# LSTM state as the loaded operand: four 32-column tiles of TensorE, with the gates' weights moving

## The chip, the cores and the metric

The kernel runs on one core of a Trainium2 chip. The core has TensorE (PE in the profile; its loads of the stationary operand are shown apart, as PEld), VectorE (DVE), ScalarE (ACT), GpSimd (POOL) and SyncE (SP), which here issues most transfers. The metric is the device time of one execution in microseconds. Before the change the median of three runs is 1354.62 us (1354.28 to 1355.16); the profiled execution took 1354.57 us, and its span from first to last instruction is 1352.8 us.

## What is computed

`x` has the shape (32, 512, 128): 32 batches of 512 nodes with 128 features. `adj` is (32, 512, 512), symmetric, of zeros and ones. Four graph layers follow each other, each after a LayerNorm and a ReLU and each added to `x`:

- layer 0: attention masked by `adj`;
- layer 1: a graph convolution whose last weight matrix comes from an LSTM;
- layer 2: four small layers with sums over neighbours in both directions;
- layer 3: a product with one weight matrix, a sum over neighbours, a bias and a PReLU.

The change is in layer 1. A convolution of the last 128 nodes of each batch gives a sequence of T = 128 steps with 128 features for each of the 32 batches, and the LSTM runs over it:

```python
def step(carry, xt):
    h, c = carry
    z = xt @ w_ih.T + b_ih + h @ w_hh.T + b_hh
    i, f, g, o = jnp.split(z, 4, axis=-1)
    c = jax.nn.sigmoid(f) * c + jax.nn.sigmoid(i) * jnp.tanh(g)
    h = jax.nn.sigmoid(o) * jnp.tanh(c)
    return ((h, c), h)
...
out = jax.nn.sigmoid(jnp.matmul(agg, lw))
```

`lw` is the LSTM's output, 128x128 for each batch, so layer 1 of every batch needs the last step. A step is a product of the 32x128 state with a 128x512 weight matrix, a few element-wise operations on 32x128 numbers, and the next step waits for them.

## The kernel before

**Stages.** Pass 1 (`pass_1`) runs for all 32 batches up to the convolution: attention for the last 128 nodes only, then the sequence goes to the tile `seq` (f_seq, 128 features on partitions x 128 steps x 32 batches). Then the LSTM (`lstm`) runs. Pass 2 (`pass_2`) does the attention of the other 384 nodes, batch by batch, and does not need the LSTM: scores (line 1256), exponentials (1259), the multiply with `adj` (1260) and the values (1265), with the query product in line 1247. `rest` does layers 1 to 3 of a batch. It can start with squares of `adj` (1317), a normalised copy of its input and a first sum over neighbours (the tile f_pg, line 1301); from line 1353, where the LSTM's result of that batch is transposed, it needs the last step. `fold` prepares weights of layer 2 between pass 2's batches.

**Order.** Nothing here is left to the order of the source. Each piece is handed to a planner (`Plan`) with an engine, a duration, a rank and what it reads and writes. `Plan.run` simulates the engines with these durations and starts, on each engine, the piece that can start first; among those that can start together the lower rank wins. The instructions are then issued in that order on each engine, and on the chip each engine works through its own queue in order. The LSTM's pieces have ranks 0 to 127, which is below `URGENT`; pass 2 has 20,000 and more, `rest` 30,000 and more. While an urgent piece is foreseen on an engine (`foresee`, `expected`), a piece of higher rank is not started if it would run into it by more than 0.2 us (line 689). Pieces of `rest` and the last `LATE` = 3 batches of pass 2 have ranks that mix them in the final stage, but nothing keeps them from starting earlier if their buffers are free. Some buffer tags are handed out strictly in the order of creation ("ar", "x", "n0" and others); the tag "mm" stands for the eight banks of PSUM.

**The LSTM's layout.** The partitions hold the features of a gate and the free axis holds the 32 batches. For each gate q the weights `w[:, W_HH + q, :]`, 128x128, are loaded and the state `seq[:, t - 1, :]`, 128x32, moves (`states`, line 1193). In fp32 each such product leaves two records of loading and two of multiplying in the profile. Gates i, f and g of four steps share one PSUM tile f_z; gate o of sixteen steps has a tile of its own, f_zo. Before use both are filled with the biases (`fill`, lines 913 and 917), and the products of the inputs are added for all steps of the tile at once (`inputs`, line 1186). A step is then:

- PE: three products of the state into f_z, then the one of gate o into f_zo (1193);
- ACT: tanh of i, f, g (1208) and of o (1225); sigmoids are computed as tanh of half the argument, and the weights and biases have been scaled for that by `halves`;
- DVE: `cell`, three instructions (1215 to 1217), gives the new cell state f_c;
- ACT: tanh of f_c (1228);
- DVE: the product with gate o is written into `seq[:, t, :]` (1229), in place of the input that is no longer needed, and the next step's products read it from there.

The biases `lstm_b` are loaded as 8 rows, turned to columns by a PE transpose (line 933), summed and scaled, and spread to `lb_row`.

Of the kernel before, what the change touches and what calls it, by code (L numbers as in the profile page):

```python
# [520 lines left out]
class Plan:  # L521
# [19 lines left out]
    def __init__(self, bufs, fifo, banks):  # L541
        self.banks = banks
        self.last = float("inf")
        self.sealed = 0
        self.ops = []
        self.bufs = bufs
        self.made = {}
        self.fifo = {t: [] for t in fifo}
# [40 lines left out]
    def run(self, tc, queues):  # L589
# [14 lines left out]
        for o in ops:  # L604
            if o.rank >= self.last:
                k, sub = divmod(o.rank - self.last, 10)
                o.rank = self.last + 12 * k - 9 * max(0, k - 28) + 200.0 - (min(behind[o], 60) if sub == 5 else behind[o] + (70 if sub == 2 else 0.0))
        free = {}
# [24 lines left out]
        def foresee(o):  # L633

            at, before = o.end, o.engine
            for _ in range(5):
                o = min((n for n in o.next if n.rank < self.URGENT), key=lambda n: n.no, default=None)
                if o is None:
                    return
                (e, (took, _)), = o.engines.items()  # L640
                at += self.lag(before, e, True)
                before = e
                expected[e] = at
                at += took
# [7 lines left out]
        def room(o):  # L652

            at = 0.0
            need = {}
            for c in o.cells:
                if c not in seen:
                    if c.tag in self.fifo and self.fifo[c.tag][turn[c.tag] + need.get(c.tag, 0)] is not c:
                        return None
                    need[c.tag] = need.get(c.tag, 0) + 1  # L660
            for t, n in need.items():
                if len(slots[t]) < n:
                    return None
                at = max(at, sorted(slots[t])[n - 1])
            return at
# [5 lines left out]
        while done < len(ops):  # L671
            best = None
            for e, cands in pools.items():
                first = None
                held = expected.get(e)
                for rank, no, o in cands:
# [10 lines left out]
                    if rank < self.URGENT:  # L687
                        held = s
                    elif held is not None and s < held < s + o.engines[e][0] - 0.2:
                        continue  # L690
# [14 lines left out]
            for c in o.cells:  # L705
# [7 lines left out]
                if c.left == 0:  # L713
                    slots[c.tag].append(c.free_at)
                    if c.tag == self.banks:
                        unused.append((c.free_at, c.place))
            for n in o.next:
                n.waits -= 1
                if n.waits == 0:
                    put(n)  # L720
# [9 lines left out]
def symmetric(ctx, tc, x, adj, weights, cols, rows, lstm_b, prelu_a, out, fail):  # L730
# [19 lines left out]
    LATE = 3  # L750
    FOLDS = (4, 7, 10, 13)
    MOVED = range(2, B - 2)
    TURN = 32
    assert D == P and N == 512

    BUFS = {"a": 2, "ar": 6, "x": 7, "xn": 5, "y": 5, "gs": 5, "inv": 4, "n0": 4, "n1": 4, "n2": 4, "n3": 4, "low": 3, "hp": 2, "dt": 2, "mm": 8, "st": 4, "mv": 4, "rs": 4, "sh": 4, "dg": 4, "dv": 4,
            "ri": 3, "th": 3, "c": 3, "cu": 2, "cv": 2, "tcn": 2}
# [99 lines left out]
    lbc = const.tile([P, 4], FP, name="f_lbc")  # L857
# [8 lines left out]
    lb = const.tile([8, P], FP, name="f_lb")  # L866
# [20 lines left out]
    w_lb = load(HEAD + 100, 4, lb, lstm_b.rearrange("s q f -> (s q) f"))  # L887
# [37 lines left out]
    def halves(q):  # L925
        half = 1.0 if q == 2 else 0.5
        nc.gpsimd.tensor_scalar_mul(w[:, W_HH + q, :], w[:, W_HH + q, :], 0.5 * half)
        if q != 2:
            nc.gpsimd.tensor_scalar_mul(w[:, W_IH + q, :], w[:, W_IH + q, :], half)
            nc.gpsimd.tensor_scalar_mul(lbc[:, q : q + 1], lbc[:, q : q + 1], half)  # L930
    lbs = plan.fixed(lbc)
    pb8 = bank("f_pb8", (P, 2, 4), whole=False)
    PE(HEAD + 110, T_TR, lambda: nc.tensor.transpose(pb8.t, lb, ident[0:8, 0:8]), [w_lb], [pb8])

    def two_biases():
        nc.vector.tensor_copy(lbc, pb8.t[:, 0, :])
        nc.vector.tensor_add(lbc, lbc, pb8.t[:, 1, :])
    DVE(HEAD + 110, 0.3, two_biases, [pb8], [lbs])
    for q in range(4):
        POOL(HEAD + 110, 0.6 if q == 2 else 1.4, lambda q=q: halves(q), [w_lstm], [lbs])  # L940
    lb_row = const.tile([P, 4 * B], FP, name="f_lb_row")
    lbrs = plan.fixed(lb_row)
    DVE(HEAD + 110, t_dve(P), lambda: nc.vector.tensor_copy(lb_row.rearrange("p (q b) -> p q b", b=B),
                                                      lbc.unsqueeze(2).to_broadcast([P, 4, B])), [lbs], [lbrs])
# [227 lines left out]

    def lstm():
        last = list(conv_ops)
        steps = []
        c = None

        def inputs(t, n, gates, name, ahead):

            g = len(gates)  # L1180
            z = bank(f"f_z{name}_{t}", (P, n, g, B), filled=True)
            row = lb_row[:, gates[0] * B : (gates[-1] + 1) * B]
            fill(2_000 + t, lambda: z.t.rearrange("p k q b -> p k (q b)"), row.unsqueeze(1).to_broadcast([P, n, g * B]), [lbrs],
                 z, conv_ops + steps[t - ahead : t - ahead + 1] if t >= ahead else conv_ops)
            for i, q in enumerate(gates):
                PE(2_000 + t, t_mm(n * B), lambda i=i, q=q: nc.tensor.matmul(
                    z.t[:, :, i, :], w[:, W_IH + q, :], seq[:, t : t + n, :], start=False, stop=(i == g - 1),
                    skip_group_check=True), [], [z])
            return z

        def states(z, k, gates, t):
            for i, q in enumerate(gates):
                nc.tensor.matmul(z.t[:, k, i, :], w[:, W_HH + q, :], seq[:, t - 1, :], start=False, stop=True,  # L1193
                                 skip_group_check=True)

        z = zo = None
        for t in range(T):
            R = t
            k = t % MANY
            if k == 0:  # L1200
                z = inputs(t, MANY, (0, 1, 2), "", MANY + 1)
            if t % (4 * MANY) == 0:
                zo = inputs(t, 4 * MANY, (3,), "o", 3)
            ko = t % (4 * MANY)
            if t:
                PE(R, 0.65, lambda z=z, k=k, t=t: states(z, k, (0, 1, 2), t), [], [z], after=last)
            th = new("th", (P, 4, B), f"f_th_{t}")
            ACT(R, 0.22, lambda th=th, z=z, k=k: nc.scalar.activation(th.t[:, :3, :], z.t[:, k, :, :], AF.Tanh), [z], [(th, 0)])  # L1208
            cn = new("c", (P, B), f"f_c_{t}")
            if t:  # L1210
                u = new("cu", (P, B), f"f_cu_{t}")
                v = new("cv", (P, B), f"f_cv_{t}")
# [10 lines left out]
            if t:  # L1223
                PE(R, 0.22, lambda zo=zo, ko=ko, t=t: states(zo, ko, (3,), t), [], [zo], after=last)
            ACT(R, 0.13, lambda th=th, zo=zo, ko=ko: nc.scalar.activation(th.t[:, 3, :], zo.t[:, ko, 0, :], AF.Tanh), [zo],
                [(th, 1)])
            tcn = new("tcn", (P, B), f"f_tcn_{t}")
            ACT(R, 0.13, lambda tcn=tcn, c=c: nc.scalar.activation(tcn.t, c.t, AF.Tanh, scale=0.5), [c], [tcn])
            last = [DVE(R, 0.09, lambda th=th, tcn=tcn, t=t: nc.vector.scalar_tensor_tensor(  # L1229
                seq[:, t, :], th.t[:, 3, :], 1.0, tcn.t, OP.add, OP.mult), [th, tcn], [])]  # L1230
# [277 lines left out]
    plan.last = 30_000  # L1508
# [84 lines left out]
```

## Time and profile before

| | before |
|---|---|
| median of three runs | 1354.62 us |
| PE busy over the span | 1329.0 us (98%) |
| DVE, ACT, POOL busy | 74%, 58%, 28% |
| mean granted clock of TensorE | 0.996 |
| LSTM, start of first tanh to start of last state | 187.0 to 509.3 us |
| line 1193, records of loading and multiplying | 1016 each |

A row of the costliest groups names the line, the engine, the operation, the tile written and the tiles read, the shapes and the count; then busy time and the mean duration; then the idle time of the engine just before, with what ended it:

```profile
L1193 PE MATMUL f_z<-f_seq,f_w 128*128 128x32 f32 x762 | 98.4, 266 | 0.4 <-DVE f_seq L1229 0.2
L1208 ACT ACTIVATE f_th<-f_z 128x96 f32<-128x96 f32 x128 | 32.0, 250 | 78.2 <-PE f_z L1193 75.3
```

The first row is the state's products for gates i, f and g: 127 steps, three gates and two records are 762. "128*128" is the part of the array that is used and 128x32 the result. PE did not stand idle ahead of them. The second row is the first tanh of each of the 128 steps, 250 ns long; of the time that ACT stood idle ahead of it, 75.3 us ended when PE had finished the products. The durations of matmuls overlap: PE takes up the next one before the last has come out at the other end, so a sum of durations is more than the time that PE was occupied.

### The profile page before, as it was taken

To read this page: it belongs to the slowest core of one execution; us is meant where nothing else is said; L and a number is where in the kernel's file an instruction comes from. 1 tells how busy PE (TensorE), PEld (TensorE's weight loads), DVE (VectorE), ACT (ScalarE), POOL (GpSimd) and SP (SyncE) were. 2 spreads that over 40 slices of the span, in tenths; PEclk is the share of its full clock that TensorE was granted. 3 is DMA by queue.
4 is the path that set the end of the run, shared out by engine and by line. 5 is a ranking of instruction groups with operands and counts; after the bars stand their busy time and mean duration, and the time that the engine had idled before them with its cause. 6 is when DMAs were issued, how large, how long until landed. Compare 5 with 4: busy or idle time off the path is not lost. (4 is left out here: it accounts for less than half of the span.)

```text
span 1352.8 us, 24316 instructions
## 1 busy us (share of the span) xinstructions
PE 1329.0 (98%) x8016; PEld 1078.1 (80%) x8018; DVE 1004.6 (74%) x3315; ACT 782.5 (58%) x1905; POOL 374.2 (28%) x689
## 2 busy tenths in 40 slices
PE   8999999999999999999999999999999999999996
PEld 6888888888888887787787787787787787787774
DVE  7988866566666678768778778788788788788644
ACT  5666644454444556566666566566566666676433
POOL 4645421111111224333233233233232232242101
PEclk9999999999999999999999999999999999999999
DMA  8888888656555535856656755756655656674211
GB/s 242 280 273 275 285 278 299 216 169 190 170 176 173 161 89 131 185 112 130 150 121 134 150 123 133 156 117 134 155 122 135 150 125 134 147 145 98 47 32 35
DMA packets 286120, 215.74 MB, mean 159 GB/s; under 512 B 135576, under 2 KB 248480, under 8 KB 285984
## 3 DMA queue, kind: packets, MB, share of 16 engines
q1 hardware_dynamic: 269088, 197.32, 53.1%
q0 software_dynamic: 16896, 16.78, 7.9%
q8 instruction: 65, 1.06, 0.3%
q14 instruction: 71, 0.58, 0.2%
HBM read 125.84 MB, written 56.75 MB: 135 GB/s over the span
## 5 line engine op out<-in xcount | busy, mean ns | idle before, releaser
L1301 PE MATMUL f_pa<-f_ar,f_y 128*128 128x512 f32 x1024 | 304.5, 431 | 0.0
L1301 PEld LDWEIGHTS f_pa<-f_ar,f_y 128*128 128x128 f32 x1024 | 190.2, 189 | 73.6 <-issue 40.1
L1407 PE MATMUL f_py<-f_wf,f_n 128*128 128x128 f32 x1280 | 174.1, 275 | 0.0
L1407 PEld LDWEIGHTS f_py<-f_wf,f_n 128*128 128x128 f32 x1280 | 164.8, 192 | 8.7 <-ACT f_n L1422 1.0
L1422 ACT ACTIVATE f_n<-f_pa,f_bcol 128x512 f32<-128x512 f32 x128 | 88.3, 690 | 132.1 <-PE f_pa L1418 131.9
L1418 PE MATMUL f_pa<-f_n,f_wf 128*128 128x512 f32 x320 | 152.8, 592 | 0.0
L1375 POOL DMA_DIRECT2D f_das<-f_ar x32 | 36.0, 1126 | 367.6 <-DVE f_ar L1344 348.6
L1283 ACT CAST f_y<-f_py 128x512 fp32r<-128x512 f32 x128 | 74.4, 581 | 78.7 <-PE f_py L1407 55.2
L1265 PE MATMUL f_po<-f_v,f_e 128*128 128x129 f32 x768 | 108.7, 279 | 1.5 <-DMA f_v<-f_dv 1.5
L1265 PEld LDWEIGHTS f_po<-f_v,f_e 128*128 128x128 f32 x768 | 98.8, 191 | 14.1 <-issue 2.7
L1193 PEld LDWEIGHTS f_z<-f_seq,f_w 128*128 128x128 f32 x762 | 96.7, 191 | 15.6 <-DVE f_seq L1229 12.7
L1414 DVE TENSOR_TENSOR f_pa<-f_pa,f_inv 128x512 f32<-128x512 f32 x128 | 88.3, 692 | 17.4 <-PE f_pa L1301 17.2
L1284 DVE TENSOR_TENSOR f_y<-f_py,f_y 128x512 fp32r<-128x512 f32 x128 | 87.0, 681 | 18.3 <-ACT f_y L1283 18.0
L1256 PE MATMUL f_s<-f_q,f_kq 128*128 128x384 f32 x256 | 99.9, 500 | 0.0
L1193 PE MATMUL f_z<-f_seq,f_w 128*128 128x32 f32 x762 | 98.4, 266 | 0.4 <-DVE f_seq L1229 0.2
L1418 PEld LDWEIGHTS f_pa<-f_n,f_wf 128*128 128x128 f32 x320 | 58.0, 189 | 46.2 <-issue 37.4
L1025 ACT ACTIVATE f_xn_c<-f_x,f_sh_c,f_rs_c 128x128 f32<-128x128 f32 x199 | 86.1, 495 | 11.9 <-DVE f_sh_c L1033 11.9
L1380 DVE SCALAR_TENSOR_TENSOR f_junk<-f_a,f_aT 128x1024 bf16<-128x1024 f32 x64 | 78.3, 1223 | 9.7 <-DMA f_aT<-f_das 8.1
L1317 ACT ACTIVATE f_ar<-f_a 128x512 fp32r<-128x512 f32 x128 | 78.8, 620 | 8.4 <-DMA f_a<-in_adj_dram 6.3
L1276 POOL COPY f_ln<-f_mv_r 128x3 f32<-128x3 f32 x32 | 9.5, 296 | 264.0 <-DVE f_mv_r L1007 255.0
L1260 DVE TENSOR_TENSOR f_e<-f_e,f_a 128x384 f32<-128x384 f32 x128 | 68.5, 551 | 14.4 <-ACT f_e L1259 13.4
L1208 ACT ACTIVATE f_th<-f_z 128x96 f32<-128x96 f32 x128 | 32.0, 250 | 78.2 <-PE f_z L1193 75.3
(204 smaller groups left out, 2921.4 us busy)
## 6 DMA issues: line engine op xcount, KB each, us to landing
f_a<-in_adj_dram SPq DMA_DIRECT2D x32, 1024.0 KB
f_a<-in_adj_dram SPq DMA_DIRECT2D x32, 768.0 KB
f_das<-f_ar POOLq DMA_DIRECT2D x32, 512.0 KB, 5.1
f_dkq<-f_kh SPq DMA_DIRECT2D x32, 448.0 KB
f_kq<-f_dkq SPq DMA_DIRECT2D x32, 448.0 KB
f_dv<-f_v SPq DMA_DIRECT2D x32, 258.0 KB
f_v<-f_dv SPq DMA_DIRECT2D x32, 258.0 KB
f_x<-in_x_dram SPq DMA_DIRECT2D x32, 256.0 KB
```

The lines of the kernel that those rows point to most:

```text
L1025: nc.scalar.activation(xn.t[:, t, :], xc.t[:, t, :], AF.Relu, bias=shift(t), scale=rstd(t))
L1193: nc.tensor.matmul(z.t[:, k, i, :], w[:, W_HH + q, :], seq[:, t - 1, :], start=False, stop=True, skip_group_check=True)
L1256: PE(R, t_mm(NR), lambda s=s, j=j: nc.tensor.matmul(s.t, kq.t[:, bass.ts(j, P)], q.t, start=True, stop=True), [kq, q], [s])
L1265: PE(R, t_mm(P), lambda t=t, j=j: nc.tensor.matmul(po.t[:, t, :], es[j].t[:, bass.ts(t, P)], v.t[:, j, :], start=(j == 0), stop=(j == NT - ...
L1284: DVE(rank, t_dve(N), lambda: nc.vector.tensor_sub(parts.t[:, :, 1, :], src.t, f32(parts.t[:, :, 0, :])), [src, (parts, 0)], [(parts, 1)])
L1301: nc.tensor.matmul(pg.t, parts.t[:, j, k, :], ar.t[:, j, :], start=(k == 0 and j == 0), stop=(k == 1 and j == NT - 1))
L1317: ACT(R, 0.62, lambda t=t: nc.scalar.activation(ar.t[:, t, :], a.t[:, t, :], AF.Square, accum_out=deg.t[:, t : t + 1]), [a], [(ar, t), (de ...
L1380: nc.vector.scalar_tensor_tensor(junk, flat(a.t[:, 2 * k : 2 * k + 2, :]), 1.0, flat(aT.t[:, 2 * k : 2 * k + 2, :]), OP.mult, OP.not_equal ...
L1407: nc.tensor.matmul(py.t[:, j, :], nodes[n].t[:, bass.ts(j, P)], wf[:, W_F[i] + c, 0, :], start=False, stop=(c == nch - 1), skip_group_chec ...
L1414: before = DVE(R, t_dve(N), lambda pa=pa: nc.vector.tensor_mul(pa.t, pa.t, inv_row.t), [inv_row], [pa])
L1418: nc.tensor.matmul(pa.t, wf[:, W_F[i] + c, 1, :], nodes[n].t, start=False, stop=(c == nch - 1), skip_group_check=True)
L1422: ACT(R, 0.57, lambda pa=pa, n=n, i=i: nc.scalar.activation(n.t, pa.t, AF.Tanh, bias=bcol[:, i : i + 1]), [pa], [n])
```

## The change

The two operands of the LSTM's products change places. The state, 128 features x 32 batches, is now loaded, and the gates' weights move. A loaded operand of 32 columns fills a quarter of the array's columns, so the array is used as four tiles of 32 columns. Tile j gets the same state and the weights of features 32j to 32j+31 of all four gates, 128 moving columns, and writes PSUM partitions 32j to 32j+31. So partitions hold (block of features, batch), and the free axis holds 4 gates x 32 features of the block; the element-wise operations keep their size, 128x32. All four gates of four steps share one tile f_z, and f_zo is gone.

The new state comes out in that layout (f_h), while the next step has to load it with features on partitions. A DVE transpose by blocks of 32x32 turns it and writes `seq[:, t, :]`.

The inputs' products can't be done for four steps at once with this layout, since each step's input would be another loaded operand. They are done by the same function, one step's worth behind the state's products of each step, for the tile that comes next. The biases now lie along the free axis and are loaded in that form; the PE transpose of the biases is gone, and sums and scaling go to POOL.

The purpose is to use the array's columns fully for a state with only 32 batches, and so to need less of PE for each step. The planner gets new durations (0.26 us for a set of four tiles, 0.1 for switching), `LATE` becomes 2, the threshold for pieces that run into an urgent one becomes 0.05 us, and one PSUM bank is kept free of pass 2 and later pieces until the LSTM has ended (`spared`, `left`).

```diff
-                    elif held is not None and s < held < s + o.engines[e][0] - 0.2:
+                    elif held is not None and s < held < s + o.engines[e][0] - 0.05:
...
-                if len(slots[t]) < n:
+                if len(slots[t]) < n + (t == self.banks and o.rank >= self.spared and self.left > 0):
...
-    LATE = 3
+    LATE = 2
...
+    T_STEP, T_SWITCH = 0.26, 0.1
...
-        def states(z, k, gates, t):
-            for i, q in enumerate(gates):
-                nc.tensor.matmul(z.t[:, k, i, :], w[:, W_HH + q, :], seq[:, t - 1, :], start=False, stop=True,
-                                 skip_group_check=True)
...
+        def products(z, k, m, h):
+            for j in range(P // TURN):
+                part = bass.ts(j, TURN)
+                nc.tensor.matmul(z.t[part, k, :, :], h, w[:, m : m + 4, part], start=False, stop=True, skip_group_check=True)
...
+            def step(z=z, coming=coming, k=k, t=t):
+                if t:
+                    products(z, k, W_HH, seq[:, t - 1, :])
+                if coming is not None:
+                    products(coming, k, W_IH, seq[:, t + MANY, :])
...
-            last = [DVE(R, 0.09, lambda th=th, tcn=tcn, t=t: nc.vector.scalar_tensor_tensor(
-                seq[:, t, :], th.t[:, 3, :], 1.0, tcn.t, OP.add, OP.mult), [th, tcn], [])]
+            h = new("h", (P, TURN), f"f_h_{t}")
+
+            def out_of(th=th, tcn=tcn, h=h, t=t):
+                nc.vector.scalar_tensor_tensor(h.t, th.t[:, 3, :], 1.0, tcn.t, OP.add, OP.mult)
+                nc.vector.transpose(seq[:, t, :], h.t)
+            last = [DVE(R, 0.31, out_of, [th, tcn], [h])]
```

## The prediction, made before the changed kernel was run

> **What bounds the kernel now.** The chain that ended last is cut off after two DVE instructions, so it says nothing. I read the busy time by stretches first, for 186 to 510 us, where the LSTM runs beside pass 2 (first f_z tanh at 187.0, last state written at 509.3).
>
> ```profile
> 292.00:346.00 54.00, 53.84 (x387) 46.23 (x385) 34.79 (x161) 25.69 (x92) 5.97 (x12) 1.00 0.62 186
> 346.00:400.00 54.00, 54.00 (x382) 46.43 (x382) 35.20 (x161) 25.64 (x90) 7.79 (x15) 1.00 0.57 174
> ...
> 510.00:560.00 50.00, 47.77 (x263) 37.17 (x262) 41.29 (x117) 32.59 (x79) 18.14 (x26) 0.97 0.62 137
> 560.00:760.00 200.00, 198.45 (x1074) 156.50 (x1073) 153.33 (x399) 126.38 (x282) 62.08 (x93) 1.00 0.61 137
> ```
>
> Columns: stretch and length; PE, PEld, DVE, ACT, POOL busy with counts; clock; DMA share; GB/s. PE is full with the LSTM and after it; DVE stands at 0.65, ACT at 0.48 and DMA at 0.6. Next, the timeline of one step (the work between it left out):
>
> ```profile
> 383.71 0.19 DVE L1229 SCALAR_TENSOR_TENSOR f_seq<-f_th,f_tcn 128x32 f32<-128x32 f32 x1 [0.35 <-ACT f_tcn L1228]
> ...
> 384.09 0.75 PEld L1193 LDWEIGHTS f_z<-f_seq,f_w 128*128 128x128 f32 x6
> 384.20 0.75 PE L1193 MATMUL f_z<-f_seq,f_w 128*128 128x32 f32 x6
> 384.76 0.30 PEld L1193 LDWEIGHTS f_zo<-f_seq,f_w 128*128 128x128 f32 x2
> ...
> 384.99 0.25 ACT L1208 ACTIVATE f_th<-f_z 128x96 f32<-128x96 f32 x1 [0.68 <-PE f_z L1193]
> ...
> 385.27 0.19 DVE L1215 SCALAR_TENSOR_TENSOR f_cu<-f_th,f_c 128x32 f32<-128x32 f32 x1 [0.76 <-ACT f_th L1208]
> 385.38 0.18 DVE L1216 SCALAR_TENSOR_TENSOR f_cv<-f_th 128x32 f32<-128x32 f32 x1
> ...
> 385.60 0.19 DVE L1217 SCALAR_TENSOR_TENSOR f_c<-f_cu,f_cv 128x32 f32<-128x32 f32 x1
> 385.88 0.23 ACT L1228 ACTIVATE f_tcn<-f_c 128x32 f32<-128x32 f32 x1 [0.47 <-DVE f_c L1217]
> ...
> 386.14 0.19 DVE L1229 SCALAR_TENSOR_TENSOR f_seq<-f_th,f_tcn 128x32 f32<-128x32 f32 x1 [0.35 <-ACT f_tcn L1228]
> ```
>
> From state to state 2.43 us pass: 0.38 to the first weight load, 0.90 to the tanh, 0.28 + 0.33 + 0.28 + 0.26 through the cell. The mean step is (509.3 − 188.0)/127 = 2.53. So **two limits lie 4% apart**: the chain of a step, and PE.
>
> PE's work in the window, by spacing of starts rather than by busy time (which overlaps): a pair of load and matmul with up to 128 moving columns takes (0.75 − 0.19)/5 = 0.112 us; one with 384 columns 0.323 (sixteen at 514.6 last 5.33, the last 0.49); with 512, 0.43. The window holds 1016 pairs of line 1193 (113.8 us), 192 and 16 of line 1186 (21.5 + 6.9), 662 of line 1265 (74.1), 275 of lines 1256 and 1247 (88.8), and folds and two early aggregates (about 14). The sum is 319 of 324 us, 142 of it the LSTM's. One batch of pass 2 is 24 × 0.112 + 10 × 0.323 = 5.9 us; 60 pairs of line 1265, 2.5 batches, fall after 510.
>
> **What the Trainium skill says.** "TensorEngine Tiling (Array Packing)", Tiling Modes, Key Properties: the tiles load and multiply in parallel, but a change of tiling mode drains TensorE. The trace of before has no tiles, so it shows neither. "TensorE: Matmul & The Clock Gate", LDWEIGHTS (loading the stationary operand): a load takes its columns divided by 1.2, in ns, so 107 for 128; the 112 ns spacing agrees. It would be 27 for 32 columns, which no row here shows. Same page, Measured speedup vs the span model: three column tiles of 32 gave 2.38×. "VectorE: DVE Perf Modes", The three transpose paths: DVE turns 32x32 blocks only, which is all the new layout needs.
>
> **The change part by part.** *Set of four tiles.* A product of the state had 4 gates × 2 records = 8 pairs, 0.90 us. It becomes 4 tiles × 2 records, again 8 pairs, each with 32 loaded and 128 moving columns. Bounds: a pair of 128 moving columns takes 0.112, so all four side by side leave 2 × 0.112 = 0.22, and none 0.90 (16 instructions at 56 ns is also what line 1193 shows, and I can't tell whether loading or issue sets that). At the page's 2.38/3 = 0.79 per tile, four give 3.2 and 0.90/3.2 = 0.28 us. I take 0.28.
>
> *Input products.* 192 + 16 pairs, 28.4 us, become 128 more sets, queued behind the state products in the same piece, so behind the instruction that the tanh waits for: PE time, not chain.
>
> *Mode switches.* Two a step. Bounds: 0, and 0.38 (twice 0.19, the shortest duration of a 32-column matmul, as its way through the array). I take 0.15, half of it ahead of the products. The LSTM on PE is then 255 × 0.28 + 127 × 0.15 = 71 + 19 = 90 us instead of 142: **52 us of PE work less**.
>
> *Chain, products.* Load to tanh is now 5 × 0.112 + 0.34. New: 7 × 0.035 + 0.34 + 0.08 (276 − 191 ns, median 128-column against shortest 32-column matmul) − 0.07 (shorter first load) + 0.07 switch = 0.67, a saving of 0.23.
>
> *Chain, turning back.* The state goes to f_h and a DVE transpose writes f_seq, and the products now wait for that one. Dependent DVE instructions start 0.22 apart (line 1216 to 1217), and the nearest row for the transpose is
>
> ```profile
> L1387 DVE STREAM_TRANSPOSE f_dT<-f_dinv 128x32 f32<-128x32 f32 x32 | 6.5, 204 | 0.0
> ```
>
> so +0.22 on the chain and 26 us more DVE in the window (0.65 to about 0.74, hidden). Behind it on DVE stand only pass 2's multiplies, which have slack. The o gate's products came last and now come with the others; its tanh runs behind the first tanh as before: nothing. Bias fills: 25 + 7 of 384 and 8 of 512 columns become 32 of 512, on engines at half load: nothing. Bias loads and sums at the head lie beside pass 1, whose PE is 96% busy: nothing. So the undisturbed step stays at 2.43 − 0.23 + 0.22 = **2.42 us**.
>
> *Disturbance.* Now 2.53 − 2.43 = 0.10 a step, from pieces of pass 2 that hold an engine when the chain's turn comes (PE's load stood idle only 31 times for the state, so mostly it came to a busy PE). The threshold for starting such a piece falls from 0.2 to 0.05 us and PE gets slack; DVE gets more work. I take 0.05: 127 steps of 2.47 are 313 us instead of 127 × 2.53 = 321, **8 us less**.
>
> *What fills PE.* A window of 316 us (three more for its ends, as now) holds 90 (LSTM) + 14 + up to 212 us of pass 2, 35 batches; only 30 are left when it begins. So the 2.5 batches after 510 can move in: LATE goes from 3 to 2, and later ranks too are started where an engine would idle. That is worth up to 2.5 × 5.9 = 14.7 us, of which I take 10. Two more early aggregates (16 pairs at some 0.2, half a fp32 pair of 512 columns): about 4 us; more must wait for the LSTM's end, since line 1353 turns its result. The rest of the kernel stays full and unchanged. Sum: 8 + 10 + 4 = 22, so 1354.6 − 22 = 1332.6, **1332 us**.
>
> **Rivals.** *A: all freed PE time is used.* PE 98% busy speaks for it; against it, 2.42 × 127 = 307 us of chain, above PE's 90 + 14 + 30 × 5.9 = 281. It needs a shorter step (2.3, if switches cost nothing and disturbance vanishes) plus more early work: 1354.6 − 52 = 1303.
>
> *B: the tiles overlap badly.* If the second record of a tile waits for its first and the tiles follow in program order, a set takes 5 × 0.107 = 0.54; the step becomes 2.47 + 0.26 = 2.73, its 127 take 347 us, +26, less the 10 and 4 that still move: 1367, slower. Without any overlap (0.90), the LSTM is 255 × 0.90 + 19 = 249 us of PE, +107, about 1455. For it: 56 ns per instruction is the closest spacing that this trace shows for fp32. Against: the page's 2.38×.
>
> *C: nothing net.* The chain grows by 0.1 (dear switches): 127 × 2.57 = 326, +5, against 14 that moves: 1346. To end level with before it must grow by 14/127 = 0.11 over 2.53, so by 0.17 over my 2.47.
>
> **How the numbers follow.** My forecast (spread 1314 to 1348, C included) has 0.66; A 0.13; B 0.17; an even result 0.04. Predicted: 1332. Below 1304 lies half of A, and above 1364 some two thirds of B, so 1304 to 1364 leaves out under 2 in 10. Faster: 0.66 + 0.13 = 0.79; same 0.04; slower 0.17.
>
> **What would show it.** The eight pairs of a set start within 0.28 us (B: 0.54 or 0.90). Load to tanh 0.67. The transpose starts 0.22 after the write of f_h, takes about 204 ns, and releases PE. Step 2.47 in the mean, LSTM over near 502 us. PE in the window at about 0.95 instead of full, DVE 0.74; fewer than 30 pairs of the value product after the LSTM's end. I am wrong if the set is above 0.4 us, if a switch costs more than 0.2, or if the late batches stay behind the LSTM.

## The result, and the profile after

The changed kernel takes 1338.9 us (median of 4 runs, 1337.5 to 1342.4) against 1354.9 (1354.3 to 1356.5, 4 runs) for the kernel before on the same chip. The ratio is 0.9884, with a 95% interval from 0.9863 to 0.9905: **16 us faster**, 7 us less of a gain than the 22 to 23 of the prediction. The profiled execution is the longest of the four (1342.4; its span is 1340.5), so its stretches are a few us longer than those of the median.

The head of the page, after. The digits are tenths of busy time and of the granted clock in 40 slices of 33.5 us:

```profile
PE 1287.5 (96%) x8829; PEld 994.2 (74%) x8830; DVE 1013.2 (76%) x3416; ACT 780.5 (58%) x1921; POOL 368.2 (27%) x689
...
PE   8999999999999937999999999999999999999996
...
PEclk9999999999999967999999999999999999999998
```

PE's busy time fell by 1329.0 − 1287.5 = 41.5 us, but the span by only 12.3: 29.2 us more of it are idle. The digits 3 and 7 say where, and the clock fell in the same two slices. The stretches (columns as in the prediction: stretch and length; PE, PEld, DVE, ACT, POOL; clock; DMA share; GB/s):

```profile
346.00:400.00 54.00, 53.84 (x575) 36.34 (x568) 42.47 (x203) 27.73 (x103) 8.89 (x18) 1.00 0.72 218
440.00:476.00 36.00, 35.89 (x380) 24.77 (x379) 27.95 (x136) 20.96 (x76) 11.33 (x20) 1.00 0.34 90
476.00:510.00 34.00, 11.79 (x116) 7.22 (x115) 16.04 (x63) 12.50 (x49) 3.51 (x8) 0.60 0.59 116
510.00:560.00 50.00, 45.06 (x251) 36.72 (x250) 39.15 (x115) 32.67 (x75) 17.62 (x29) 0.93 0.51 110
560.00:760.00 200.00, 200.00 (x1069) 156.81 (x1068) 151.86 (x393) 123.93 (x273) 53.68 (x83) 1.00 0.58 128
```

Beside the LSTM PE is as full as before, until pass 2 runs out at 476. From there to the LSTM's end (last transpose at 504.4) it has the steps and nothing else. In the stretch from 476 to 510 it is busy for 11.79 of 34 us, at a clock of 0.60, where it was full before. That stretch alone holds 22.2 of the 29.2 us. From 560 us on PE is as full as before.

The row groups of the new products and of the transpose:

```profile
L1193 PE MATMUL f_z<-f_w,f_seq 128*32 128x128 f32 x2040 | 84.1, 283 | 22.2 <-DVE f_seq L1241 16.5 <-ACT f_ar L1329 4.5
L1241 DVE STREAM_TRANSPOSE f_seq<-f_h 128x32 f32<-128x32 f32 x128 | 27.0, 211 | 4.8
```

PE now does stand idle for the state (16.5 us, more than half of it in one wait that is shown below; before it was 0.2). One step in the middle of pass 2, from the timeline, other work left out:

```profile
381.58 0.16 DVE L1240 SCALAR_TENSOR_TENSOR f_h<-f_th,f_tcn 128x32 f32<-128x32 f32 x1
381.77 0.21 DVE L1241 STREAM_TRANSPOSE f_seq<-f_h 128x32 f32<-128x32 f32 x1
...
382.04 0.38 PEld L1193 LDWEIGHTS f_z<-f_w,f_seq 128*32 128x32 f32 x16 [0.64 <-DVE f_seq L1241]
382.04 0.64 PE L1193 MATMUL f_z<-f_w,f_seq 128*32 128x128 f32 x16
...
382.53 0.25 ACT L1219 ACTIVATE f_th<-f_z 128x96 f32<-128x96 f32 x1
...
382.61 0.30 PEld L1268 LDWEIGHTS f_s<-f_q,f_kq 128*128 128x128 f32 x2 [0.20 <-issue]
...
383.72 0.19 DVE L1240 SCALAR_TENSOR_TENSOR f_h<-f_th,f_tcn 128x32 f32<-128x32 f32 x1
```

Read it as follows. Sixteen pairs (a set for the state, a set for a later step's input) take 0.64 us, the last one 0.27, so they start (0.64 − 0.27)/15 = 0.025 us apart in the mean. That mean hides a pattern. The same view cut off at 382.10 shows the first four alone:

```profile
382.04 0.32 PE L1193 MATMUL f_z<-f_w,f_seq 128*32 128x128 f32 x4
```

The first of them lasts 0.30 us, so these four start 0.007 us apart. (They are one in each tile: run 4 will show that one tile alone starts a pair only every 0.109 us.) The next fours start at 382.17, 382.28 and 382.39. So **four pairs start together every 0.11 us**, and a set of eight needs 0.22 us and not 0.28. From the load to the tanh 0.49 us pass instead of 0.90. Then the loader stands idle for 0.20 us, with nothing to wait for that the profile shows, before it loads the first full-width operand of pass 2: the way back from the tiles. The same 0.20 stands in each of the 120 such places between 190 and 476 us. From f_h to f_h 2.14 us pass, which is the shortest step of the run.

And this is the place where most of the tail goes wrong, 4 us behind the end of pass 2:

```profile
473.46 4.02 SPq L1389 DMA_TRANSPOSE f_aT<-f_das  x1
...
479.94 0.25 ACT L1219 ACTIVATE f_th<-f_z 128x96 f32<-128x96 f32 x1 [1.10 <-PE f_z L1193]
...
485.64 1.97 SPq L1389 DMA_TRANSPOSE f_aT<-f_das  x1
485.70 1.23 DVE L1392 SCALAR_TENSOR_TENSOR f_junk<-f_a,f_aT 128x1024 bf16<-128x1024 f32 x1 [6.39 <-DMA f_aT<-f_das]
...
486.85 0.19 DVE L1226 SCALAR_TENSOR_TENSOR f_cu<-f_th,f_c 128x32 f32<-128x32 f32 x1
...
489.00 1.08 PE L1193 MATMUL f_z<-f_w,f_seq 128*32 128x128 f32 x16 [8.90 <-DVE f_seq L1241]
```

The tanh of i, f, g starts at 479.94, but the cell comes 6.9 us later. Between them, in DVE's queue, stands `differ` (line 1392), a test of `rest` whether `adj` is symmetric; it compares a part of `adj` with a transposed copy, and waits 6.39 us for the transposing transfer. SP had issued that one at 473.46, 12 us before the test could start (the issue at 485.64 is the next batch's). The planner's order had put the test ahead of the cell in DVE's queue, and a queue is worked through in order. In this gap PE idles for 8.90 us. Then the sixteen pairs take 1.08 us, the last one 0.42, and the fours start 0.21 us apart, twice as far as before: the granted clock has fallen to 0.50, at 482 us, in the gap. It stays so to the LSTM's end.

### The profile page after: what moved, and what is told of

It is laid out like the page before. It is cut to its first block, busy times and chain, and to the rows that moved or that the text cites. A ratio compares the mean times of both kernels' runs of the same rounds, so it can differ in the third digit from the quotient of the medians.

```text
span 1340.5 us, 26042 instructions
## 1 busy us (share of the span) xinstructions
PE 1287.5 (96%) x8829; PEld 994.2 (74%) x8830; DVE 1013.2 (76%) x3416; ACT 780.5 (58%) x1921; POOL 368.2 (27%) x689
## 5 line engine op out<-in xcount | busy, mean ns | idle before, releaser
L1193 PE MATMUL f_z<-f_w,f_seq 128*32 128x128 f32 x2040 | 84.1, 283 | 22.2 <-DVE f_seq L1241 16.5
L1193 PEld LDWEIGHTS f_z<-f_w,f_seq 128*32 128x32 f32 x2040 | 49.3, 110 | 60.7 <-issue 15.5
L840 DVE COPY f_gT<-f_pg 128x512 f32<-128x512 f32 x28 | 19.4, 692 | 80.1 <-PE f_pg L1313 79.9
L1313 PE MATMUL f_pg<-f_ar,f_xp_c 128*128 128x512 f32 x256 | 74.3, 416 | 3.7 <-ACT f_xp_c L1303 3.7
```

The costliest lines, as they stand in the source:

```text
L1193: nc.tensor.matmul(z.t[part, k, :, :], h, w[:, m : m + 4, part], start=False, stop=True, skip_group_check=True)
L1313: nc.tensor.matmul(pg.t, parts.t[:, j, k, :], ar.t[:, j, :], start=(k == 0 and j == 0), stop=(k == 1 and j == NT - 1))
```

## The experiments

Medians in us; "before" was run beside each call and had medians of 1353.9 to 1354.9.

| run | what it is | median | ratio to before, 95% |
|---|---|---|---|
| | the changed kernel | 1338.9 | 0.9884 [0.9863, 0.9905] |
| 1 | first bias fills only after pass 1 | 1338.9 | 0.989 [0.9874, 0.9906] |
| 2 | symmetry tests behind the LSTM | 1337.7 | 0.988 [0.9861, 0.9898] |
| 3 | no transpose in the step | 1314.9 | 0.9713 [0.9698, 0.9728] |
| 4 | all four products in one tile | 1490.8 | one run |
| 5 | the kernel before with all planner settings of the change | 1364.2 | 1.0072 [1.0055, 1.0089] |
| 6 | the changed kernel with threshold 0.2 and LATE 3 | 1362.6 | 1.0055 [1.0038, 1.0072] |
| 7 | run 2 with LATE 0 | 1328.3 | 0.9809 [0.979, 0.9829] |
| 8 | run 2 with small matmuls in the last steps | 1333.3 | 0.9841 [0.9825, 0.9858] |
| 9 | the changed kernel with threshold 0.2 alone | 1359.5 | 1.0039 [1.0024, 1.0054] |
| 10 | the changed kernel with LATE 3 alone | 1333.1 | 0.9838 [0.9823, 0.9853] |
| 11 | the kernel before with threshold 0.05 alone | 1364.0 | 1.0079 [1.0063, 1.0095] |
| 12 | runs 7 and 8 in one | 1327.4 | 0.9799 [0.9786, 0.9812] |

### What the products gained: runs 4 and 3

**Run 4: one tile.** Is this spacing the work of four tiles side by side, or just what a load of 32 columns costs?

```diff
-                nc.tensor.matmul(z.t[part, k, :, :], h, w[:, m : m + 4, part], start=False, stop=True, skip_group_check=True)
+                nc.tensor.matmul(z.t[bass.ts(0, TURN), k, :, :], h, w[:, m : m + 4, part], start=False, stop=True, skip_group_check=True)
```

> All four products of a set write the same 32 partitions, that is, use the same column tile, with the same loads and moving columns; three quarters of the results are left out. The order of instructions is that of the changed kernel. Theory, the 25 ns spacing of pairs comes from four tiles working side by side: [...]a set takes 0.86 us instead of 0.20, each step grows by 1.3 us of PE work, and the kernel is slower than before the change, some 1450 us or more. Rival, the spacing comes from the short loads of 32 columns alone: the set stays at 0.2 to 0.3 us and the time at 1339 to 1350.

Measured: 1490.8 us. Its timeline, the same sixteen pairs:

```profile
382.55 1.67 PEld L1193 LDWEIGHTS f_z<-f_w,f_seq 128*32 128x32 f32 x16 [1.09 <-issue]
382.58 1.91 PE L1193 MATMUL f_z<-f_w,f_seq 128*32 128x128 f32 x16 [0.50 <-DVE f_seq L1241]
```

The last matmul lasts 0.27 here too, so (1.91 − 0.27)/15 = 0.109 us pass from pair to pair and 0.87 for a set. With four tiles the same 0.109 us pass from one four to the next, and a set takes 0.22: four tiles work side by side, with the whole factor of four. With one tile the LSTM's last tanh comes at 651.3 instead of 503.0. So the new layout without the tiles is the prediction's rival B at its far end, and somewhat beyond it.

**Run 3: no transpose.** What is a shorter chain worth? The new state is written in the turned layout straight into `seq`, so that the next steps multiply numbers in the wrong places; one DVE instruction less stands in every step.

```diff
-            h = new("h", (P, TURN), f"f_h_{t}")
...
-                nc.vector.scalar_tensor_tensor(h.t, th.t[:, 3, :], 1.0, tcn.t, OP.add, OP.mult)
-                nc.vector.transpose(seq[:, t, :], h.t)
-            last = [DVE(R, 0.31, out_of, [th, tcn], [h])]
...
+                nc.vector.scalar_tensor_tensor(seq[:, t, :], th.t[:, 3, :], 1.0, tcn.t, OP.add, OP.mult)
+            last = [DVE(R, 0.09, out_of, [th, tcn], [])]
```

> Leaves out the DVE transpose of the state: it is written into f_seq in the turned layout, and planned with 0.09 us. Theory, the chain of a step sets the LSTM's length: the step becomes 0.22 to 0.23 us shorter (2.36 to about 2.14 before the tail), the LSTM some 25 us shorter, and the kernel 15 to 28 us shorter. Rival, PE's work in the window sets it: step and time change by less than 5 us.

Measured: 1314.9 us, 24 less than the changed kernel; the row of the first tanh and two stretches:

```profile
L1219 ACT ACTIVATE f_th<-f_z x128: 242/250/251, 188.8 to 462.2; 128x96 f32<-128x96 f32 x128
...
346.00:400.00 54.00, 53.42 (x598) 36.00 (x602) 38.28 (x189) 28.32 (x110) 11.04 (x18) 1.00 0.64 202
...
476.00:510.00 34.00, 31.11 (x164) 23.23 (x164) 27.75 (x77) 20.26 (x50) 11.72 (x20) 1.00 0.59 139
```

The mean step falls from (503.0 − 192.4)/127 = 2.45 to 2.15 (up to 475 us, without the hole, from 2.38 to 2.14), and no hole opens at 476, since the LSTM ends before pass 2 does. PE is full in the middle in both kernels, and yet 0.21 us of DVE work a step are worth 24 us. **The chain, not PE's work, sets the LSTM's length now.** The run also takes 27 us of work from DVE; that this relieves other work than the chain is not ruled out, but the steps shrink by about what leaves the chain. A full PE in a stretch did not mean that PE's work set the end: here PE was full early with work that it then lacked late.

### The hole at 480: runs 1, 2 and 8

**Run 1: the fills.** The first suspicion was PSUM: the two first bias fills are made at 54 us and hold two of the eight banks through pass 1.

```diff
-                 [lbrs], z, steps[t - MANY - 3 : t - MANY - 2] if t > MANY + 2 else [])
+                 [lbrs], z, steps[t - MANY - 3 : t - MANY - 2] if t > MANY + 2 else conv_ops)
```

> The first two bias fills of the LSTM (f_z of steps 0 and 4) wait for the convolutions, as the fills did before the change. In the changed kernel both are made at 54 us and hold two of the eight PSUM banks until the LSTM starts at 191.0 us (185.7 before the change). Theory, banks: pass 1 gets its banks back, the LSTM's products start at 186 to 187 us and the kernel takes 4 to 5 us less than the changed one (1334). Rival, the four bias loads on the SyncE queue at 21 to 43 us are what delays pass 1: the start stays at 190 to 191 us and the time at 1338 to 1339.

Measured: 1338.9 us, no change, and PE still stood idle for 8.7 us at the same place. The theory of the banks fell. The LSTM's first products start at 188.3 here and at 191.0 in the profile of the changed kernel. In runs 2, 4, 7 and 10, whose instructions stand in the changed kernel's order on every engine up to 400 us, they start at 186.5 to 188.5. So of the five us that the changed kernel's profile loses ahead of the LSTM (185.7 to 191.0), 2.5 to 4.5 are a difference between executions.

**Run 2: the symmetry tests behind the LSTM.**

```diff
-        differ_ops.append(DVE(R + 2, 1.2, differ, [a, aT], []))
+        differ_ops.append(DVE(R + 2, 1.2, differ, [a, aT], [], after=lw_after))
```

> The symmetry test of an early batch (tile f_junk, DVE) waits for the LSTM's end. In the changed kernel one stands in DVE's queue ahead of a cell at 480 us and waits 6.4 us for a transposing transfer; PE stands idle for 8.9 us and its clock falls to half for the rest of the LSTM. Theory, queued wait: no gap, the last ten steps take 2.2 to 2.3 us each, the LSTM ends some 8 to 9 us earlier (495 to 496), and the kernel takes 6 to 9 us less (1330 to 1333). Rival, the gap is hidden by work that PE does later anyway, or the early batches only shift their cost behind the LSTM: LSTM earlier, but the time within 2 us of 1339.

Measured: 1337.7 us, only 1.2 less and within the spread, as the rival had it. The hole is gone and the LSTM ends at 494.4, 10 us earlier, but:

```profile
480.00:510.00 30.00, 13.68 (x96) 9.10 (x89) 18.54 (x74) 13.33 (x49) 5.10 (x10) 0.50 0.33 97
...
494.32 1.18 DVE L1392 SCALAR_TENSOR_TENSOR f_junk<-f_a,f_aT 128x1024 bf16<-128x1024 f32 x1
...
498.08 1.22 DVE L1392 SCALAR_TENSOR_TENSOR f_junk<-f_a,f_aT 128x1024 bf16<-128x1024 f32 x1
499.23 0.69 DVE L1379 SCALAR_TENSOR_TENSOR f_x<-f_sg,f_x 128x512 f32<-128x512 f32 x1
...
504.10 1.15 PE L827 MATMUL f_xt_c<-f_ident,f_xn_c 128*128 128x128 f32 x4 [5.03 <-DVE f_xn_c L1025]
```

The four tests now stand together in DVE's queue exactly where the LSTM's result comes out, ahead of the first batch's next step (line 1379), whose result PE needs; PE waits 5.03 us and starts on it at 504.1, still at half clock. But this is not where the ten us were lost. In the changed kernel PE starts that step (line 827) only at 518.7, 14.6 us later. The lead shrinks behind it: at the 65th of the products that line 1313 adds into f_pa (32 a batch) it is 4.7 us (557.0 against 561.7), and the two profiled spans end 4.6 apart. So the rest was lost between 505 and 560 us, where the first batches are started; which wait took it there is not shown.

**Run 8: holding the clock.** Run 2 with four matmuls of zeros behind the products of each of the last 12 steps.

```diff
+            if t >= T - 12:
+                for i in range(4):
+                    warm_up(50_000 + t, 0.216, f"f_wl_{t}_{i}", ops_pe)
```

> The kernel of e2 with four matmuls of zeros (bf16, 512 columns, about 0.22 us each) behind the products of each of the last twelve steps, where PE has nothing else. In e2 the granted clock is 0.50 from 480 to 510 us; the last eight steps take 2.5 us instead of 2.2 and the first products of the last stage run at half speed. Theory, the clock costs 3 us in the LSTM's tail and 2 to 4 after it: clock near 1.0 there, LSTM's end 2 to 3 us earlier, kernel 3 to 6 us shorter than e2 (1332 to 1335). Rival, the stage after the LSTM waits for DVE, ACT and transfers: the end of the LSTM moves, the time stays within 2 us of 1337.7.

Measured: 1333.3 us, 4.4 below run 2, with all other instructions in run 2's order on every engine; the same stretch has a clock of 0.85 instead of 0.50:

```profile
480.00:510.00 30.00, 17.85 (x128) 10.23 (x128) 19.01 (x74) 14.20 (x52) 6.87 (x13) 0.85 0.33 96
```

So the clock was worth 4 us. But the LSTM's end moved by 0.7 us only (last tanh at 492.0 instead of 492.7), where 2 to 3 had been expected; the 65th product into f_pa comes 3.6 us earlier, so most of the gain lies behind the LSTM.

The Trainium skill, "TensorE: Matmul & The Clock Gate", What's actually happening, says that TensorE's clock is gated by how busy it has lately been. These traces agree: in run 2 the clock falls to 0.50 at 476.7 us, 3 us after the last product of pass 2, when only the steps are left, and here, with the small matmuls between the steps, not before 501.1.

### The planner's settings: runs 5, 6, 9, 10, 11, 7 and 12

**Run 5: the settings without the products.** The kernel before with the threshold, `LATE`, the free bank and the gap in `foresee`.

```diff
-            at, before = o.end, o.engine
+            at, before = o.end + o.gap, o.engine
...
-                if len(slots[t]) < n:
+                if len(slots[t]) < n + (t == self.banks and o.rank >= self.spared and self.left > 0):
...
-                    elif held is not None and s < held < s + o.engines[e][0] - 0.2:
+                    elif held is not None and s < held < s + o.engines[e][0] - 0.05:
...
-    LATE = 3
+    LATE = 2
...
-    plan.last = 30_000
+    plan.last, plan.spared = 30_000, 20_000
```

> The kernel before with only the planner's part of the change: LATE 2, the threshold of 0.05 us, the spared bank and the gap in foresee; the LSTM's products stay as they were. Theory, the products bring the gain: within 4 us of 1354 (LSTM's end near 509, or a few us earlier for the smaller threshold with as much pass 2 left over). Rival, the planner's settings bring a good part of it: 1345 or less.

Measured: 1364.2 us, 9.3 slower than before; neither theory had that size.

**Run 6: the products without the two numbers.** The changed kernel with threshold 0.2 and `LATE` 3.

> The changed kernel with LATE 3 and the threshold of 0.2 us as before the change (the spared bank stays). Theory, the products bring the gain: the step is a little longer (2.36 to 2.40), one more batch of pass 2 (5.9 us) may stay behind the LSTM, 1339 to 1347. Rival, the settings bring a good part: 1348 or more.

Measured: 1362.6 us: the new products with the old numbers are slower than the kernel before. Neither half of the change gains anything alone. Runs 9 to 11 split this.

**Run 9: threshold alone, in the changed kernel.**

```diff
-                    elif held is not None and s < held < s + o.engines[e][0] - 0.05:
+                    elif held is not None and s < held < s + o.engines[e][0] - 0.2:
```

> The changed kernel with the old threshold of 0.2 us alone (LATE stays 2). With both old settings the time was 1362.6, LSTM steps took 2.64 us in the mean and pass 2 had run out at 449. Theory: the threshold does it, because a piece that starts just ahead of an urgent one pushes every step back, and the many steps of pass 2 that get in eat up what should fill PE at the end; expected 1350 to 1360, mean step above 2.55. Rival: the LATE setting does it, and this one stays within 4 us of the changed kernel, 1335 to 1343, with a mean step of 2.46.

Measured: 1359.5 us, so in the changed kernel the threshold is worth 20.6 us. The row of the first tanh and the end of the LSTM:

```profile
L1219 ACT ACTIVATE f_th<-f_z x128: 241/251/253, 188.5 to 523.3; 128x96 f32<-128x96 f32 x128
...
186.00:450.00 264.00, 263.42 (x2732) 185.77 (x2731) 202.43 (x951) 141.16 (x497) 54.84 (x103) 1.00 0.74 234
450.00:530.00 80.00, 41.43 (x476) 27.07 (x475) 43.63 (x187) 31.18 (x127) 10.54 (x20) 0.66 0.52 118
```

The step takes 2.64 us in the mean. PE is full up to 450, because more of pass 2 is let in ahead of each step; then 80 us follow with PE half empty.

**Run 10: LATE alone, in the changed kernel** (`LATE = 3`).

> The changed kernel with LATE 3 alone (threshold stays 0.05). LATE 0 instead of 2 was worth 9.4 us, so one batch was worth some 4.7 us. Theory: this loses one batch's worth, 1341 to 1348, and the steps stay as in the changed kernel (mean 2.46 up to where pass 2 ends). Rival: LATE carries the loss of the old settings, and this one comes out at 1355 or more.

Measured: 1333.1 us, 5.8 *less* than the changed kernel; neither theory had the sign. With this setting the tests fall elsewhere in DVE's queue (two at 475 to 478, two at 505 to 508), no wait for a copy shows, and the LSTM's last tanh comes at 493.8. Two batches of pass 2 (48 value pairs) are now left behind the LSTM instead of one, but 24 records of early aggregates come before its end instead of 16. So `LATE` 2 cost time here. Whether the place of the tests or the third aggregate is the reason stays open.

**Run 11: threshold alone, in the kernel before.**

> The kernel before with the threshold of 0.05 us alone: old products, LATE 3, no bank kept free. With all of the new settings it took 1364.2, 9.6 us more than before, with shorter steps and more of pass 2 left behind the LSTM. Theory: with PE full, a threshold that leaves PE idle ahead of each step costs work that is lost, so this too is slower, by 4 to 10 us (1358 to 1364), the LSTM ends earlier than 509, and more than 120 pairs of the value product come after 480. Rival: the bank kept free cost it, and this one stays within 2 us of before.

Measured: 1364.0 us, 9.2 slower, the whole of run 5. The same edit has the other sign with the old products. The groups of PE up to the LSTM's end, first of before (186 to 510), then of this run (186 to 497.6), each with the loads for the state first:

```profile
L1193 PEld LDWEIGHTS f_z<-f_seq,f_w 128*128 128x128 f32 x762 | 96.7, 191 | 15.6 <-DVE f_seq L1229 12.7
L1265 PE MATMUL f_po<-f_v,f_e 128*128 128x129 f32 x662 | 95.5, 280 | 0.0
L1256 PE MATMUL f_s<-f_q,f_kq 128*128 128x384 f32 x221 | 87.3, 503 | 0.0
...
L1301 PE MATMUL f_pg<-f_ar,f_xp_c 128*128 128x512 f32 x16 | 4.7, 413 | 0.0
```

```profile
L1193 PEld LDWEIGHTS f_z<-f_seq,f_w 128*128 128x128 f32 x762 | 95.4, 191 | 23.4 <-DVE f_seq L1229 22.0
L1265 PE MATMUL f_po<-f_v,f_e 128*128 128x129 f32 x588 | 84.5, 279 | 0.0
L1256 PE MATMUL f_s<-f_q,f_kq 128*128 128x384 f32 x198 | 79.3, 505 | 0.0
```

The LSTM's last tanh comes at 495.8 instead of 508.1, 12.3 us earlier. But 74 value pairs, three batches of 5.9 us, and the 16 records of the early aggregate (4.7 us) have not been done by then: 22 us more are left behind. The difference, 22 − 12, is about the loss of 9. The loader stood idle for the state 22.0 us instead of 12.7, and these 9.3 us more have the size of the loss. With PE's work as the bound, holding PE back for the chain only costs work.

**Run 7: LATE 0 on top of run 2**, so that no batch of pass 2 is ranked into the final stage.

> The kernel of e2 (the symmetry test waits for the LSTM's end) with LATE 0: no batch of pass 2 is held for the last stage. In e2 PE runs empty from 476 us on while one batch, 5.9 us of PE, is still done after the LSTM. Theory, the lost gain is PE time that stays unused at the LSTM's end: the batch moves into the gap and the kernel takes 4 to 6 us less than e2 (1332 to 1334). Rival, that batch filled waits of the first batches of the last stage: the time stays within 2 us of 1337.7 or grows.

Measured: 1328.3 us, 9.4 below run 2, more than the 4 to 6 expected. The last value pairs lie at 476.3 instead of one batch behind the LSTM. The planner's order differs from run 2's from some 420 us on, in more than this batch, so not all of the 9.4 need be the batch's.

**Run 12: runs 7 and 8 in one.**

> The changed kernel with the symmetry test behind the LSTM, LATE 0, and the four small matmuls behind each of the last 12 steps, that is, the last two experiments in one. Alone they came to 1328.3 and 1333.3, 9.4 and 4.4 us below the kernel they were made from (1337.7). If they act on different stretches of time the sum holds: 1323 to 1325. If LATE 0 takes the same idle time of PE that the small matmuls keep warm, nothing or 1 to 2 us is added: 1326 to 1330.

Measured: 1327.4 us (1326.0 to 1329.4), 1.0 below run 7 and within its spread (1327.3 to 1331.1). The second theory held: with the last batch in the window there is little idle time left to keep warm, although the clock is better (0.89 in 480 to 510). It is the fastest full kernel here, 0.9799 [0.9786, 0.9812] of before; that it beats run 7 is not shown.

## Why the prediction was right and wrong

The direction and the mechanism held: 1332 was foretold and 1338.9 measured, inside the range. The gain was 16 us, some seven tenths of the 22.6. Its steps, one by one:

| step | predicted | measured |
|---|---|---|
| set of four tiles | 0.28 us | 0.22 |
| a switch, both ways | 0.15 a step | about 0.2 (0.09 on the way in, 0.11 on the way back) |
| load to tanh | 0.67 | 0.49 in the step shown, 0.50 in the mean |
| state to load | 0.38 + 0.22 = 0.60 | 0.46 in the step shown, 0.69 in the mean |
| f_h to transpose; its duration | 0.22; 204 ns | 0.22 in the mean; 211 ns |
| undisturbed step (measured: the shortest) | 2.42, from 2.43 | 2.14, from 2.24 |
| mean step | 2.47, from 2.53 | 2.38, from 2.53, up to 475; 2.45 in all |
| disturbance (mean less shortest) | 0.05, from 0.10 | 0.24, from 0.29 |
| LSTM's length | 8 us less | 10 less in the profiled run |
| PE in the window | about 0.95 | 0.93: full to 476, then 0.35 |
| DVE in the window | 0.74 | 0.73 |
| late batches | 10 us | 36 of 60 pairs moved, 1.5 batches, 8.9 us |
| two more early aggregates | 4 us | none: 16 records, as before |
| head | nothing | 1 to 5 us later, mostly between executions |

**The set and the way to the tanh were mis-sized to the safe side.** The step of 3.2-fold overlap, taken from three tiles, failed: run 4 gives 4, and the set takes 0.22 us, the prediction's own lower bound. From load to tanh the eighth pair starts 0.15 us after the first and not 7 × 0.035 = 0.245, and the tanh comes 0.34 us after that; the other three terms (0.08, −0.07 and 0.07) came to nothing. The 0.08 set the median of one form against the shortest record of the other; the medians are 276 ns for 32 moving columns before and 273 for 128 after. The Trainium skill, "TensorE: Matmul & The Clock Gate", Wait — 56ns, not 53.3ns?, has a floor of about 25 ns between starts. The mean of 0.025 us looks like it, but it is not that: here starts in different tiles come 7 ns apart, and what holds the spacing is the 0.109 us of each tile, the same as in run 4.

**The switch** was sized about right. A full-width pair of 128 columns is followed by the next one of its kind after 0.112 us, by the first one in a tile after 0.20 (0.32 and 0.42 for 384 columns). On the way back the next full-width pair starts 0.22 us behind the start of the last four, instead of 0.11.

**"I take 0.05" for the disturbance rests on a step that was not undisturbed.** The 2.43 us that the prediction read are those of a common step. Two lines of before, from the same stretch, show a shorter one:

```profile
391.01 0.16 DVE L1229 SCALAR_TENSOR_TENSOR f_seq<-f_th,f_tcn 128x32 f32<-128x32 f32 x1
...
393.27 0.19 DVE L1229 SCALAR_TENSOR_TENSOR f_seq<-f_th,f_tcn 128x32 f32<-128x32 f32 x1 [0.35 <-ACT f_tcn L1228]
```

This step takes 2.26 us, and the shortest of all 2.24. So the disturbance before was 0.29 us and not 0.10, and the change left 0.24 of it; it was not halved. In the mean over the steps up to 475 us, the way from load to tanh fell by 0.43 us (0.93 to 0.50), where 0.23 had been forecast. The way from state to load grew by 0.32 (0.37 to 0.69), where the forecast had 0.22; the 0.09 of the switch into the tiles is a likely part of that, but not shown apart. The rest of the step fell by 0.05. Together that is 0.15 us, where 0.06 had been forecast.

What keeps the disturbance from growing is the threshold. With the old one the mean step is 2.61 (run 9: 96 steps instead of 105 between 190 and 440 us). I had treated it as a small term that comes along with the products; it is worth 20.6 us, more than the whole gain.

**The LSTM's 8 us came out near in part by luck.** Steps 0.15 us shorter would have made it some 19 us shorter, and in run 2, which has no hole, its first and last tanh lie 18 us closer than before (302.9 against 321.1). The hole at 480 took 9 of them back, and the prediction had no hole.

**"What fills PE" was counted, but not placed in time.** The sum said that some 212 us of pass 2 fit and 35 batches could run where 30 are left: so PE must run dry before the LSTM ends. I spread that idle share evenly ("about 0.95"), and gave it no price. It came in one piece at the end, since the planner starts what can start. Past that point the clock fell (run 8: 4.4 us), and the symmetry test's wait for its transfer stood bare in the chain (8.9 us). What this wait alone cost in time is not shown: run 2, without it, is 1.2 us faster, within the spread, but it also moves the tests behind the LSTM. In the profiled executions the span's −12.3 us are +5.3 ahead of the LSTM, 323.7 → 313.6 = −10.1 for the LSTM, and 843.4 → 835.9 = −7.5 behind it. There the prediction had 14, 10 for batches and 4 for aggregates. The batches that moved should have given 8.9; the slow, empty stretch after 500 may have taken the rest, which is not shown.

**The 4 us for early aggregates** failed: no more of them were started than before. `LATE` is a part of what held them, since run 10 starts 24 records with `LATE` 3; the rest was not tested.

**The rivals.** A (all freed PE time used) fails on 22 us of idle PE in one stretch. Its reason, a shorter step, was right, as run 3 shows from the other side. B falls with the set's 0.22 us; its far end, by its own sum (1354.6 + 107), is 1462 and not 1455. C's time (1346) lies as near to the median as the forecast does, but not its cause: the chain grew shorter, not longer.

## What to carry to other kernels

Freeing an engine that is full moves the bound to whatever stood next, here a chain that lay close by; then every setting that was tuned for the old bound has to be looked at again, for it may change its sign (the threshold: −20.6 us with the new products, +9.2 with the old). Where a long chain runs beside a fixed stock of filling work, ask when the stock runs out, not only whether it fits: past that point each delay of the chain is bare, and the clock may fall too. And a chain that ends earlier is not yet a kernel that does: of the ten us that run 2 took out of the LSTM only 1.2 arrived in the time. To judge how much a step is disturbed, compare its mean with the shortest steps of the same run, not with one step picked from the middle.

## What the runs showed of the hardware that was not expected

- Four column tiles of 32, with fp32 operands and 128 moving columns, start a pair each within 0.02 us (0.007 from one to the next), and the next four 0.109 us later. In one tile a pair starts every 0.109 us (run 4). The overlap is complete. A single load of 32 columns still shows as 105 to 110 ns at full clock.
- The way back from tiles to full width left the loader idle for 0.20 us, in all 120 places between 190 and 476 us. The way in delays the first start by 0.09 us.
- With only sixteen or eight pairs every 2.2 to 2.5 us TensorE's clock fell to a half (0.50 in 480 to 510 us of run 2); four small matmuls a step held it at 0.85.
